# Attention on one core: seven pairs of exps' tiles added by DMAs, and a unit's side work in four blocks

## The chip, the cores and the metric

The kernel runs on one core of a Trainium2 chip. The metric is the device time of one execution in microseconds (us). TensorE (PE) multiplies, VectorE (DVE) and ScalarE (ACT) work elementwise, GpSimd (POOL) adds tiles and issues DMAs of its own, and SyncE (SP) issues the other DMAs.

## What is computed

x is 8 × 2048 × 256 and adj is 2048 × 2048, mostly zeros. Two layers follow each other, each with a residual and a LayerNorm:

```
x = layernorm(x + gcn(x, adj, ...))      # aggregation, two linears with batch norms
qkv = x @ W                              # 4 heads of 64
scores = q @ k.T / 8 + where(adj == 0, -inf, 0)
x = layernorm(x + softmax(scores) @ v)
```

The change touches only the second layer, the masked attention. Its softmax needs, for every query and head, the sum of the exps over all 2048 keys.

## The kernel before, in words

The attention works in 64 units: for each batch b (8), each pair of heads hp (2) and each chunk c of 512 queries (4). A unit has NT = 16 steps, one for each tile of 128 keys; g counts steps over all units. The order of the instructions on TensorE, VectorE, ACT and GpSimd is the order of the program text (the names in IN_ORDER), so each engine's queue can be read off the main loop at the end of attention().

One step g does the following. TensorE computes the scores of step g + 3 (scores, L838, tile st in PSUM; LEAD is 3). VectorE adds the mask (mask_scores, L850) and ACT takes the exp in place (exps, L856); the result is a tile prob of 128 keys × 2 heads × 512 queries, 512 KB, from a ring of 13. Then the step's side work is issued, then TensorE multiplies the prob of step g with v (weigh, L868, into out_ps), and add_up gives GpSimd the task of adding the tile to acc. In a unit's last step weigh comes before the masking, and finish_out copies and adds the two halves of out_ps (ACT L883, DVE L884), before that step's masking is queued.

The sums over keys: GpSimd adds the first NT − on_pe(u) tiles of a unit into acc. finish_sums then lets TensorE multiply acc, and each of the last on_pe(u) tiles, with ones (L895), which sums over the 128 partitions. on_pe is 1 in units 0 to 60 and 4 in units 61 to 63.

Side work is registered with at_step(u, j, f, ...): it runs in unit u at step int(j), in the order of j within the step. Its TensorE part stands between two groups of the step, and this text calls the side work of one step a block. It consists of:

- project (three for a unit: Q on w = 0, K on w = 1, L777; V on w = 2, L791), at the steps in PROJECT;
- finish_sums, finish_turn_sums (L909), finish_turn (L922) and finish (VectorE, L930) for the unit that ended before;
- in the four units in which a chunk of the next batch is made ready: norm, for two halves (y turned by TensorE, L711, then added to x on VectorE, L719, in add_y, with the LayerNorm statistics behind it), root (GpSimd), apply (ACT), and turn, for two halves (x1 turned by TensorE, L740, then copied to x1t by ACT, L746).

All of these use PSUM tiles named pm, from the pool ps_m with two buffers, in turn. A tile of it can be written again when its reader is done. The scores have two buffers (st) and out_ps one[...].

Before the change, a unit that prepares a chunk has blocks at step 0 (second y half, Q), 4 (sums), 6 (turned sums, K, turned output), 10 (first y half, V, first x1 half) and 13 (second x1 half). A unit that prepares none has those at 0, 4, 6 and 10 alone.

Of the kernel before, what the change touches and what calls it, by code (L numbers as in the profile page):

```python
# [8 lines left out]
F32 = mybir.dt.float32  # L9
U8 = mybir.dt.uint8  # L10
AF = mybir.ActivationFunctionType
ALU = mybir.AluOpType
# [14 lines left out]
def tile_gcn_then_masked_attention(  # L27
# [15 lines left out]
    nc = tc.nc  # L43
    ENG = mybir.EngineType
    PSUM = bass.MemoryType.PSUM
    P = 128
# [4 lines left out]
    NT = N // P  # L51
# [3 lines left out]
    CH = 512  # L55
    NCH = N // CH
# [140 lines left out]
    with tc.tile_pool(name="bt7", bufs=1, side="right") as bp7, tc.tile_pool(  # L197
        name="stage", bufs=2, side="right"
    ) as sp, tc.tile_pool(name="stage1", bufs=1, side="right") as sp1, tc.tile_pool(
        name="pst", bufs=4, space=PSUM  # L200
# [17 lines left out]
        for n, t in enumerate(order):  # L218
# [7 lines left out]
            j, m = divmod(t, HT)  # L226
            k, q = divmod(m, TPC)
            here = slice(q * P, (q + 1) * P)
            for g in range(NT // 4):
# [4 lines left out]
                i, m0 = divmod(4 * g, HT)  # L234
# [46 lines left out]
    with tc.tile_pool(  # L281
        name="psa", bufs=4, space=PSUM
    ) as psa, tc.tile_pool(name="psh", bufs=3, space=PSUM) as psh, tc.tile_pool(
        name="psd", bufs=1, space=PSUM
# [94 lines left out]
        for v, (k, b, d) in enumerate(units):  # L379
            first, last = v == 0, v == len(units) - 1  # L380
            turn = not last and units[v + 1][0] != k
            w = v + 1
# [99 lines left out]
        for n, (name, size) in enumerate((("h1", [P, NH, CH]), ("dbc", [P, N]))):  # L482
            t = lp.tile(size, F32, name=name)
            t = t if n else t.rearrange("p a b -> p (a b)")
# [156 lines left out]
    IT = BR // P  # L641
    NU = B * HP * NCH
# [34 lines left out]
    class Layer1Input:  # L677
# [37 lines left out]
        def add_y(self, b, c, half, pm, xt):  # L715
            tiles = range(IT * half, IT * (half + 1))
            here = slice(tiles[0], tiles[-1] + 1)
            t = self.x1[b, c]
            nc.vector.tensor_add(t[:, here], pm, xt[:, here])  # L719
            if half == 0:  # L720
                self.ln[b, c] = LayerNorm(self.pool, t)
            self.ln[b, c].stats(tiles)

        def root(self, b, c):
            self.ln[b, c].root(range(TPC))
# [83 lines left out]
    def attention():  # L809


        with tc.tile_pool(
# [9 lines left out]
            units = [(b, hp, c) for b in range(B) for hp in range(HP) for c in range(NCH)]  # L822
            probs, accs, outs, ots, sts, pms = {}, {}, {}, {}, {}, {}

            def on_pe(u):

                return 4 if u >= NU - NCH + 1 else 1

            def scores(g):
                u, j = divmod(g, NT)  # L830
# [40 lines left out]
                        )  # L871

            def add_up(g):
                u, j = divmod(g, NT)
                if j == 1:
                    accs[u] = ap_.tile([P, 2, CH], F32, name="acc")
                    nc.gpsimd.tensor_add(accs[u], probs[g - 1], probs[g])  # L877
                elif 1 < j < NT - on_pe(u):
                    nc.gpsimd.tensor_add(accs[u], accs[u], probs[g])  # L879

            def finish_out(u):
                ots[u] = ap_.tile([P, CH], F32, name="ot")
# [73 lines left out]
            def at_step(u, j, f, *args):  # L956
                tasks = side.setdefault((u, int(j)), [])
                tasks.append((j, f, args))
                tasks.sort(key=lambda task: task[0])

            per_b = HP * NCH
            for u in range(NU):
                b, hp, c = units[u]
                at_step(u + 1, 4, finish_sums, u)
                at_step(u + 1, 6, finish_turn_sums, u)
                at_step(u + 1, 6.2, finish_turn, u)
                at_step(u + 1, 6.2, finish, u, 0)
                at_step(u + 1, 7, finish, u, 1)
                if u == NU - 2:
                    for half in range(2):  # L970
                        at_step(u + 1, 8.3 + half, inp.emit_stats, b, c, half)
                        at_step(u + 1, 13 + half, inp.emit, b, c, half)
                    at_step(u + 1, 10.5, inp.root, b, c)
                elif u == NU - 1:
                    for half in range(2):
                        at_step(u + 1, 6.3 + half, inp.emit_stats, b, c, half)
                        at_step(u + 1, 6.4 + half, inp.root_half, b, c, half)
                        at_step(u + 1, 8 + half, inp.emit_half, b, c, half)
                    at_step(u + 1, 10, count_sums)
                elif hp == HP - 1:  # L980
                    for half in range(2):
                        at_step(u + 1, 10.3 + 3 * half, inp.emit_stats, b, c, half)
                        at_step(u + 2, 3 + half, inp.emit, b, c, half)
                    at_step(u + 2, 2, inp.root, b, c)

            PROJECT = (0.1, 6.1, 10.1)

            def project_at(u, b, hp, c):  # L990
                for w in range(3):
                    at_step(u, PROJECT[w], inp.project, b, hp, c, w)

            for b in range(B):
                u0 = b * per_b
                if b:
                    project_at(u0, b, 0, NCH - 1)
                for c in range(NCH):
                    project_at(u0 + 1 + c, b, 1, c)
                    if b + 1 == B:  # L1000
                        continue
                    u = u0 + 3 + c
                    at_step(u, 1, inp.load_y, b + 1, c)
                    at_step(u, 5, inp.load_x, b + 1, c)
                    for o in range(NO):
                        at_step(u, 5 + o, inp.bn, b + 1, c, o)
                    at_step(u, 10, inp.norm, b + 1, c, 0)
                    at_step(u + 1, 0, inp.norm, b + 1, c, 1)
                    at_step(u + 1, 4, inp.root, b + 1, c)
                    for half in range(2):  # L1010
                        at_step(u + 1, 7 + half, inp.apply, b + 1, c, half)
                        at_step(u + 1, 10.2 + 3 * half, inp.turn, b + 1, c, half)
                    if c < NCH - 1:
                        project_at(u + 2, b + 1, 0, c)

# [13 lines left out]
            with tc.manual_schedule(engines=IN_ORDER):  # L1029
                for c in range(NCH):  # L1030
                    inp.yt[0, c] = y0[c]
                    inp.x1[0, c] = ip.tile([P, TPC, D], F32, name="x1", bufs=NCH + 3)
                    for o in range(NO):
                        inp.bn(0, c, o)

                def ready(c):
                    pm = ps_s.tile([P, TPC, D], F32, name="st")
                    for half in range(2):
                        pmh = pm[:, half * IT : (half + 1) * IT, :]
                        inp.turn_y(0, c, half, pmh)  # L1040
                        inp.add_y(0, c, half, pmh, x0[c])
                    inp.root(0, c)

                def halves(f, c):
                    for half in range(2):
                        f(0, c, half)

                for c in range(NCH - 1):
                    ready(c)
                halves(inp.apply, 0)  # L1050
                halves(inp.turn, 0)
                halves(inp.apply, 1)
                inp.project(0, 0, 0, 1, k_on_act=True)
                inp.project(0, 0, 0, 0)
                ready(NCH - 1)
                right.close()
                ap_ = inp.y_pool = late.enter_context(
                    tc.tile_pool(name="attn", bufs=2, side="right", reuse_waits="tile")
                )
                inp.project(0, 0, 0, 2)  # L1060
                halves(inp.turn, 1)
                for g in range(LEAD):
                    mask_scores(g, scores(g))
                    exps(g)
                    if g == 1:
                        inp.project(0, 0, 1, 1)
                        halves(inp.apply, 2)
                for g in range(NU * NT):
                    u, j = divmod(g, NT)
                    ahead = g + LEAD < NU * NT  # L1070
                    if ahead:
                        st = scores(g + LEAD)
                    if j == NT - 1:
                        weigh(g)
                        finish_out(u)
                    if ahead:
                        mask_scores(g + LEAD, st)
                        exps(g + LEAD)
                    for _, f, args in side.get((u, j), ()):
                        f(*args)  # L1080
                    if j < NT - 1:
                        weigh(g)
                    add_up(g)
                for u in (NU, NU + 1):
                    for j in range(NT):
                        for _, f, args in side.get((u, j), ()):
                            f(*args)

    def attention_with_maxima():

        with tc.tile_pool(name="full", bufs=2) as ap_, tc.tile_pool(
# [9 lines left out]
            for b in range(B):  # L1101
                for c in range(NCH):
                    inp.load_y(b, c)
                    inp.load_x(b, c)
                    for o in range(NO):
                        inp.bn(b, c, o)
                    for half in range(2):
                        inp.norm(b, c, half)
                    inp.root(b, c)
                    for half in range(2):  # L1110
                        inp.apply(b, c, half)
                    for half in range(2):
                        inp.turn(b, c, half)
# [99 lines left out]
```

## Time and profile before

| | |
|---|---|
| time, median of 3 runs | 3622.35 us (3622.21 to 3624.46) |
| profiled execution | 3624.1 us, granted TensorE clock 0.995 |
| PE, POOL, DVE, ACT busy | 99%, 76%, 55%, 45% of the span |
| GpSimd adds into acc, L879 and L877 | 823 + 64, mean 2.37 us |
| sums on TensorE, L895 | 584 instructions for prob, 512 for acc |
| VectorE masking, L850 | 1024, mean 1.22 us |
| ACT exp, L856 | 1024, mean 1.06 us |
| a 512 KB store, out_dram<-x | 2.9 us from issue to landing |

A matmul of this type of data appears as two instructions, so a tile multiplied with ones has 8 of them. The mean of one instruction on TensorE says little, since four of the small tiles run beside each other; the timeline, with the start of one group after the other, is the better view. The busy shares are over the whole span. The attention begins near 1265 us, and in it GpSimd is busy nine tenths of the time.

### The profile page before, as it was taken

The page shows a single profiled execution, that of the slowest core. Times are in us where ns is not written, and L with a number is a line of the kernel's source. Part 1 is how long each engine was busy: PE and PEld are TensorE (multiplying, and loading weights), DVE is VectorE, ACT ScalarE, POOL GpSimd, SP SyncE. Part 2 cuts the span into 40 slices and gives each one's busy share as a digit, 9 for nine tenths or more (in the row PEclk, how much of TensorE's full clock was granted, in tenths as well). Part 3 has the DMA queues.
Part 4 walks back from the last instruction along what each step waited for, and adds up shares of the span by engine and source line. Part 5 has one row for each costly group of instructions (what it writes and reads, how often), then busy time and mean ns, then how long its engine had stood idle before and what let it go on. Part 6 is the DMA issues. An engine that isn't in the chain of part 4 may idle for free.

```text
span 3624.1 us, 55802 instructions
## 1 busy us (share of the span) xinstructions
PE 3585.2 (99%) x23055; PEld 1486.7 (41%) x23055; DVE 1988.9 (55%) x2929; ACT 1642.7 (45%) x2036; POOL 2761.0 (76%) x1461
## 2 busy tenths in 40 slices
PE   8999999999999899999999999999999999999998
PEld 5444444444444443433343433343343334343333
DVE  6212141221146656766766676676676677676666
ACT  5101100110135455665665665565566566556555
POOL 3543263424247678999999999999999999999997
PEclk9999999999999899999999999999999999999999
DMA  9122232231256300000010010010001001000000
GB/s 338 66 73 87 81 134 81 76 99 29 81 197 261 136 13 7 24 30 13 19 42 13 13 36 24 13 36 25 7 24 42 4 23 35 13 13 26 12 1 26
DMA packets 132777, 205.82 MB, mean 57 GB/s; under 512 B 6928, under 2 KB 113952, under 8 KB 122016
## 3 DMA queue, kind: packets, MB, share of 16 engines
q1 hardware_dynamic: 132048, 196.11, 15.8%
q0 software_dynamic: 288, 4.98, 0.4%
q8 instruction: 183, 3.00, 0.3%
q10 hardware_dynamic: 176, 1.06, 0.1%
q14 instruction: 82, 0.67, 0.1%
HBM read 126.62 MB, written 75.51 MB: 56 GB/s over the span
## 4 chain that ended last, share of the span: by engine, by line
PE 97%; DVE 1%; DMA 0%; ACT 0%; POOL 0%; issue 0%; POOLq 0%; ACTq 0%; SPq 0%; DVEq 0%
PE out_ps L868 25%; PE st L838 24%; PE pa L333 21%; PE pm L777 6%; PE ph L366 5%; PE pa L543 5%; PE pm L791 3%; PE pm L895 2%; PE pm L711 1%; PE pm L740 1%; PE pm L922 1%; PE ps L233 1%; PE pm L909 1%; PE ph L588 1%; DMA a<-in_adj_dram 0%; PE pc L243 0%
## 5 line engine op out<-in xcount | busy, mean ns | idle before, releaser
L879 POOL TENSOR_TENSOR acc<-acc,prob 128x1024 f32<-128x1024 f32 x823 | 1948.6, 2368 | 96.5 <-ACT prob L856 39.3
L850 DVE SCALAR_TENSOR_TENSOR prob<-mask,st 128x1024 f32<-128x1024 uint8 x1024 | 1242.7, 1219 | 605.3 <-PE st L838 551.2
L856 ACT ACTIVATE prob<-prob 128x1024 f32<-128x1024 f32 x1024 | 1082.4, 1057 | 943.7 <-DVE prob L850 923.6
L868 PE MATMUL out_ps<-prob,v 64*64 64x512 f32 x8192 | 1077.1, 596 | 1.7 <-DVE ot L884 1.7
L838 PE MATMUL st<-qt,kt 64*64 64x512 f32 x8192 | 1062.9, 589 | 0.1
L333 PE MATMUL pa<-t,x 128*128 128x512 f32 x1792 | 773.6, 594 | 2.7 <-ACT x L309 2.7
L838 PEld LDWEIGHTS st<-qt,kt 64*64 64x64 f32 x8192 | 312.6, 133 | 566.5 <-issue 527.0
L333 PEld LDWEIGHTS pa<-t,x 128*128 128x128 f32 x1792 | 341.4, 191 | 432.9 <-issue 428.9
L868 PEld LDWEIGHTS out_ps<-prob,v 64*64 64x64 f32 x8192 | 284.9, 132 | 511.5 <-issue 412.7
L414 POOL TENSOR_TENSOR ag<-ag,dbc 128x512 f32<-128x512 f32 x16 | 20.2, 1264 | 486.4 <-DVE ag L413 454.8
L370 ACT ACTIVATE h<-ph,b1s 128x512 f32<-128x512 f32 x112 | 76.9, 687 | 404.4 <-PE ph L366 404.4
L777 PE MATMUL pm<-x1t,wq 128*128 128x512 f32 x512 | 247.1, 606 | 0.7 <-ACT x1t L746 0.7
L394 ACT COPY ag<-pa 128x512 f32<-128x512 f32 x16 | 9.4, 586 | 423.1 <-PE pa L333 409.6
L366 PE MATMUL ph<-ag,w1s 128*128 128x512 f32 x448 | 193.4, 592 | 0.0
L877 POOL TENSOR_TENSOR acc<-prob 128x1024 f32<-128x1024 f32 x64 | 151.3, 2364 | 20.4 <-ACT prob L856 19.2
L672 ACT ACTIVATE x<-x,ln_nm,ln_rs 128x256 f32<-128x256 f32 x256 | 137.5, 586 | 8.0 <-POOL ln_nm L668 8.0
L371 DVE BATCH_NORM_STATS2 st<-h 128x6 f32<-128x512 f32 x112 | 76.8, 691 | 99.1 <-ACT h L370 99.1
L791 PEld LDWEIGHTS pm<-wq,x1t 128*128 128x128 f32 x1024 | 119.2, 192 | 28.5 <-issue 26.8
L366 PEld LDWEIGHTS ph<-ag,w1s 128*128 128x128 f32 x448 | 85.1, 190 | 107.1 <-issue 106.9
L791 PE MATMUL pm<-wq,x1t 128*128 128x128 f32 x1024 | 128.4, 278 | 0.0
L777 PEld LDWEIGHTS pm<-x1t,wq 128*128 128x128 f32 x512 | 88.1, 192 | 95.1 <-issue 88.3
L303 POOL TENSOR_TENSOR x<-x,dinv 128x1024 f32<-128x1024 f32 x60 | 116.8, 1968 | 0.0
(137 smaller groups left out, 2427.0 us busy)
## 6 DMA issues: line engine op xcount, KB each, us to landing
x<-in_x_dram SPq DMA_DIRECT2D x92, 512.0 KB, 4.2
h_d<-h SPq DMA_DIRECT2D x28, 1024.0 KB, 3.9
t<-h_d SPq DMA_DIRECT2D x28, 1024.0 KB, 8.0
a<-in_adj_dram SPq DMA_DIRECT2D x16, 1024.0 KB, 5.1
y_d<-ag SPq DMA_DIRECT2D x32, 512.0 KB, 2.6
out_dram<-x SPq DMA_DIRECT2D x31, 512.0 KB, 2.9
yt<-y_d SPq DMA_DIRECT2D x28, 512.0 KB, 3.2
bt_d<-t SPq DMA_DIRECT2D x4, 2048.0 KB, 13.2
```

The costliest lines, as they stand in the source:

```text
L333: nc.tensor.matmul(pa, s.t[:, m, :], t[:, m, :], start=(m == 0), stop=(m == HT - 1))
L366: nc.tensor.matmul(ph, w1s[:, d, f * P : (f + 1) * P], ag[:, d, :], start=(d == 0), stop=(d == ND - 1),)
L543: nc.tensor.matmul(py, w[:, f, :], t[:, f, :], start=(f == 0), stop=(f == 1))
L672: nc.scalar.activation(self.t[:, i, :], self.t[:, i, :], AF.Identity, bias=self.nm[:, i : i + 1], scale=self.rs[:, i : i + 1],)
L777: nc.tensor.matmul(pm, wq[:, d, wcols], xt[:, d, cols], start=(d == 0), stop=(d == ND - 1))
L791: nc.tensor.matmul(pm[:, j * P : (j + 1) * P], xt[:, d, t * P : (t + 1) * P], wq[:, d, wcols], start=(d == 0), stop=(d == ND - 1),)
L838: nc.tensor.matmul(st[r * HD : (r + 1) * HD, h, :], kt[hs, j * P + r * HD : j * P + (r + 1) * HD], qt[hs, cols], start=True, stop=True,)
L850: nc.vector.scalar_tensor_tensor(p, mask[:, j, cols][:, None, :].to_broadcast([P, 2, CH]), MASKED, st, op0=ALU.mult, op1=ALU.add,)
L856: nc.scalar.activation(probs[g], probs[g], AF.Exp)
L868: nc.tensor.matmul(outs[u][hs, r, :], inp.qkv[b, hp][2][rs, j, hs], probs[g][rs, h, :], start=(j == 0), stop=(j == NT - 1),)
L877: nc.gpsimd.tensor_add(accs[u], probs[g - 1], probs[g])
L879: nc.gpsimd.tensor_add(accs[u], accs[u], probs[g])
```

## The change

It has two parts. First, GpSimd no longer adds every tile by itself: tiles 0 and 1, 2 and 3, and so on to 12 and 13 (PAIRS) are added pairwise by accumulating DMAs, issued by GpSimd at the pair's second step. The add of the pair's sum into acc is queued four steps after. With this GpSimd has eight adds in a unit for fourteen, and on_pe goes to 0 in all units but the last: TensorE multiplies acc alone with ones.

Second, the side work is put together in fewer blocks: both y halves stand around the Q projection at step 0, both x1 halves around the V projection at step 11, and the statistics of y get a method of their own, stats_y, at steps 1 and 2. The sums move to step 5, beside the K projection, and the turned sums and output to step 8. Loads, batch norm and output move to match.

```diff
             t = self.x1[b, c]
             nc.vector.tensor_add(t[:, here], pm, xt[:, here])
+
+        def stats_y(self, b, c, half):
             if half == 0:
-                self.ln[b, c] = LayerNorm(self.pool, t)
-            self.ln[b, c].stats(tiles)
+                self.ln[b, c] = LayerNorm(self.pool, self.x1[b, c])
+            self.ln[b, c].stats(range(IT * half, IT * (half + 1)))
...
+            PAIRS = range(0, NT - 2, 2)
+
             def on_pe(u):
-                return 4 if u >= NU - NCH + 1 else 1
+                return 4 if u == NU - 1 else 0
...
             def add_up(g):
                 u, j = divmod(g, NT)
-                if j == 1:
-                    accs[u] = ap_.tile([P, 2, CH], F32, name="acc")
-                    nc.gpsimd.tensor_add(accs[u], probs[g - 1], probs[g])
-                elif 1 < j < NT - on_pe(u):
+                here = NT - on_pe(u)
+                if j - 1 in PAIRS and j < here:
+                    nc.gpsimd.dma_start(probs[g - 1], probs[g], accum_op=ALU.add)
+                elif PAIRS[-1] + 1 < j < here:
                     nc.gpsimd.tensor_add(accs[u], accs[u], probs[g])
+
+                v, i = divmod(g - 5, NT)
+                if v < 0 or i not in PAIRS[1:] or i + 1 >= NT - on_pe(v):
+                    return
+                if i == PAIRS[1]:
+                    accs[v] = ap_.tile([P, 2, CH], F32, name="acc")
+                    nc.gpsimd.tensor_add(accs[v], probs[g - 7], probs[g - 5])
+                else:
+                    nc.gpsimd.tensor_add(accs[v], accs[v], probs[g - 5])
...
-                at_step(u + 1, 4, finish_sums, u)
-                at_step(u + 1, 6, finish_turn_sums, u)
-                at_step(u + 1, 6.2, finish_turn, u)
-                at_step(u + 1, 6.2, finish, u, 0)
-                at_step(u + 1, 7, finish, u, 1)
+                at_step(u + 1, 5, finish_sums, u)
+                at_step(u + 1, 8, finish_turn_sums, u)
+                at_step(u + 1, 8.1, finish_turn, u)
+                at_step(u + 1, 8.2, finish, u, 0)
+                at_step(u + 1, 9, finish, u, 1)
...
-                        at_step(u + 1, 10.3 + 3 * half, inp.emit_stats, b, c, half)
-                        at_step(u + 2, 3 + half, inp.emit, b, c, half)
-                    at_step(u + 2, 2, inp.root, b, c)
-            PROJECT = (0.1, 6.1, 10.1)
+                        at_step(u + 1, 12 + 2 * half, inp.emit_stats, b, c, half)
+                        at_step(u + 2, 6.3 + half, inp.emit, b, c, half)
+                    at_step(u + 2, 3, inp.root, b, c)
+            PROJECT = (0.1, 5.1, 11.1)
...
-                    at_step(u, 1, inp.load_y, b + 1, c)
-                    at_step(u, 5, inp.load_x, b + 1, c)
+                    at_step(u, 2, inp.load_y, b + 1, c)
+                    at_step(u, 8, inp.load_x, b + 1, c)
                     for o in range(NO):
-                        at_step(u, 5 + o, inp.bn, b + 1, c, o)
-                    at_step(u, 10, inp.norm, b + 1, c, 0)
-                    at_step(u + 1, 0, inp.norm, b + 1, c, 1)
-                    at_step(u + 1, 4, inp.root, b + 1, c)
+                        at_step(u, 11.3 + 2 * o, inp.bn, b + 1, c, o)
                     for half in range(2):
-                        at_step(u + 1, 7 + half, inp.apply, b + 1, c, half)
-                        at_step(u + 1, 10.2 + 3 * half, inp.turn, b + 1, c, half)
+                        at_step(u + 1, 0.2 * half, inp.norm, b + 1, c, half)
+                        at_step(u + 1, 1 + 1.5 * half, inp.stats_y, b + 1, c, half)
+                        at_step(u + 1, 8.5 + half, inp.apply, b + 1, c, half)
+                        at_step(u + 1, 11 + 0.2 * half, inp.turn, b + 1, c, half)
+                    at_step(u + 1, 4.5, inp.root, b + 1, c)
```

The first batch, which is made ready before the units begin, calls stats_y behind each norm half, as before.

More of the change, by code (lines that the diff above doesn't have):

```diff
@@ L963, in attention @@
                 b, hp, c = units[u]
-                at_step(u + 1, 4, finish_sums, u)
-                at_step(u + 1, 6, finish_turn_sums, u)
-                at_step(u + 1, 6.2, finish_turn, u)
-                at_step(u + 1, 6.2, finish, u, 0)
-                at_step(u + 1, 7, finish, u, 1)
+                at_step(u + 1, 5, finish_sums, u)
[3 more added lines that the diff above has]
+                at_step(u + 1, 9, finish, u, 1)
                 if u == NU - 2:
                     for half in range(2):
-                        at_step(u + 1, 8.3 + half, inp.emit_stats, b, c, half)
+                        at_step(u + 1, 9.3 + half, inp.emit_stats, b, c, half)
                         at_step(u + 1, 13 + half, inp.emit, b, c, half)
@@ L975, in attention @@
                     for half in range(2):
[L976 to L979, printed above, removed]
+                        at_step(u + 1, 8.3 + half, inp.emit_stats, b, c, half)
+                        at_step(u + 1, 8.4 + half, inp.root_half, b, c, half)
+                        at_step(u + 1, 10 + half, inp.emit_half, b, c, half)
+                    at_step(u + 1, 12, count_sums)
                 elif hp == HP - 1:
                     for half in range(2):
-                        at_step(u + 1, 10.3 + 3 * half, inp.emit_stats, b, c, half)
-                        at_step(u + 2, 3 + half, inp.emit, b, c, half)
-                    at_step(u + 2, 2, inp.root, b, c)
-            PROJECT = (0.1, 6.1, 10.1)
+                        at_step(u + 1, 12 + 2 * half, inp.emit_stats, b, c, half)
+                        at_step(u + 2, 6.3 + half, inp.emit, b, c, half)
+                    at_step(u + 2, 3, inp.root, b, c)
+            PROJECT = (0.1, 5.1, 11.1)
             def project_at(u, b, hp, c):
                 for w in range(3):
-                    at_step(u, PROJECT[w], inp.project, b, hp, c, w)
+                    early = 1 if w == 2 and (hp, c) == (0, NCH - 1) else 0
+                    at_step(u, PROJECT[w] - early, inp.project, b, hp, c, w)
             for b in range(B):
@@ L1041, in ready @@
                         inp.add_y(0, c, half, pmh, x0[c])
+                        inp.stats_y(0, c, half)
                     inp.root(0, c)
@@ L1108, in attention_with_maxima @@
                         inp.norm(b, c, half)
+                        inp.stats_y(b, c, half)
                     inp.root(b, c)
```

## Prediction

> **What bounds the kernel now.** I read the chain of work that ended last first:
>
> ```profile
> PE 97%; DVE 1%; DMA 0%; ACT 0%; POOL 0%; issue 0%; POOLq 0%; ACTq 0%; SPq 0%; DVEq 0%
> ```
>
> TensorE alone sets the end. The change lies in the attention (from about 1265 us to the end), so I read TensorE's timeline there, over one unit in which the next batch is prepared. Columns: start, duration, engine, line, operation, tiles, count.
>
> ```profile
> 2019.30 1.04 PE L838 MATMUL st<-qt,kt 64*64 64x512 f32 x8
> 2020.27 0.66 PE L711 MATMUL pm<-ident,yt 128*128 128x128 f32 x4
> 2020.76 1.88 PE L777 MATMUL pm<-x1t,wq 128*128 128x512 f32 x4
> 2022.57 1.09 PE L868 MATMUL out_ps<-prob,v 64*64 64x512 f32 x8
> ...
> 2029.60 0.64 PE L895 MATMUL pm<-prob,ones 128*32 128x256 f32 x8
> 2030.05 0.61 PE L895 MATMUL pm<-acc,ones 128*32 128x256 f32 x8
> 2030.60 1.09 PE L868 MATMUL out_ps<-prob,v 64*64 64x512 f32 x8
> ...
> 2044.24 1.95 PE L791 MATMUL pm<-wq,x1t 128*128 128x128 f32 x16
> 2046.03 0.60 PE L740 MATMUL pm<-ident,x 128*128 128x128 f32 x4
> 2046.56 1.09 PE L868 MATMUL out_ps<-prob,v 64*64 64x512 f32 x8
> ...
> 2050.90 1.04 PE L838 MATMUL st<-qt,kt 64*64 64x512 f32 x8
> 2051.87 0.66 PE L740 MATMUL pm<-ident,x 128*128 128x128 f32 x4
> 2052.45 1.09 PE L868 MATMUL out_ps<-prob,v 64*64 64x512 f32 x8
> 2053.36 1.04 PE L838 MATMUL st<-qt,kt 64*64 64x512 f32 x8
> ```
>
> There is no bracket with an idle time: everything starts as the work before it ends. So the time is the sum of TensorE's work, and a change can shorten it only by removing TensorE work, and lengthens it by every wait it puts into TensorE's queue. Last, what the other queues do beside it (DVE, then ACT):
>
> ```profile
> 2020.16 0.69 DVE L884 TENSOR_TENSOR ot<-out_ps,ot 128x512 f32<-128x512 f32 x1 [1.90 <-ACT ot L883]
> 2020.77 2.34 DVE L850 SCALAR_TENSOR_TENSOR prob<-mask,st 128x1024 f32<-128x1024 uint8 x2
> 2023.03 0.68 DVE L719 TENSOR_TENSOR x<-pm,x 128x512 f32<-128x512 f32 x1
> ```
>
> ```profile
> 2045.20 1.06 ACT L856 ACTIVATE prob<-prob 128x1024 f32<-128x1024 f32 x1 [0.19 <-DVE prob L850]
> 2046.23 0.59 ACT L798 COPY v<-pm 128x512 f32<-128x512 f32 x1
> ```
>
> The reader is to see that the add of a y half at a unit's first step (L719) ends at 2023.71, long after its transposes, because a sum and two maskings stand before it; and that the first copy out of PSUM in the block at step 10 ends at 2046.82, because an exp stands before it. Today nothing on TensorE waits for either.
>
> **What the Trainium skill says.** "DMA: Bandwidth & Descriptors", section "SWDGE vs HWDGE vs iDMA": accumulation in a DMA is to be had from GpSimd alone, whose software writes the descriptors. So each added DMA takes GpSimd time. The trace has two DMAs of GpSimd, 0.97 us (wq, L632) and 0.58 us (mask, L633). "Collectives: The Full Stack", section "The bandwidth ceiling: the fold count and why AG ≠ RS ≠ AR": a reducing transfer reads two sources through the same ring and so runs at about half a copy's rate; no accumulating DMA is in the trace of before. "TensorEngine Tiling (Array Packing)", section "Key Properties": a change of the tiling mode drains TensorE. The trace agrees: after a block of side work the L868 group takes 0.16 us more than 0.86 on the chain of waits (1.02).
>
> **The change, part by part.**
>
> *Fewer tiles summed on TensorE.* finish_sums puts exps' tiles through ones: one in units 0 to 60, four in 61 to 63, 73 in all (the row of prob,ones has x584, 8 for each). Afterwards only unit 63 keeps its four, so 69 go. One costs 2030.05 − 2029.60 = 0.45 us; a five-tile group at the end takes 2.30 us on the chain, 0.46 each. 69 × 0.45 = 31 us, all on the bounding engine: **−31.0**.
>
> *GpSimd.* A unit had 14 adds at 2.43 us (19.48 us for 8 in a row), 34 us; it gets 8 adds (19.5) and 7 DMA issues at 0.58 to 0.97 each (4 to 7 us; I take 1), plus 1.8 us of LayerNorm roots: 28 us of a unit of 35.5 to 37.5. The list of waits has no TensorE row that waits for GpSimd, so this is worth nothing; it makes the first part possible. The accumulation (512 KB): a store of that size lands in 2.9 us here; the skill's fit of 2.0 us plus bytes over 436 GB/s ("Anatomy of one DMA"), with the bytes twice, gives an estimate of 4.4 us; upper bound 5.8, twice the store. I take 4.4. The add that needs it stands four steps later (4 × 1.72 = 6.9 us or more), and behind it GpSimd's next adds and issues. The last add of a unit comes after step 1 of the next one, ends by step 3, and finish_sums (the only TensorE work behind it) is at step 5. A tile of exps comes back after 13 steps and its masking runs three steps ahead: tile 0 is wanted at step 10, its add stands at step 7. Cost: 0.
>
> *Blocks.* The unit above has five blocks of side work; the fifth is the lone x1 half at 2051.87. It costs 2053.36 − 2050.90 = 2.46 against 1.72 for a bare step: 0.74. Afterwards the two x1 halves take the first and the last place around the V projection, where a y half and an x1 half were (no difference), and a y half goes behind the Q projection at step 0. Appended transposes cost 0.43: L791 to the next L868 is 2.32 with them (2044.24 to 2046.56) and 1.89 without (2007.92 to 2009.81). Net 0.31 in each unit that has such a block: 7 batches × 4 chunks = 28. **−8.7**. The other moves leave four blocks as four: 0, since TensorE does the same work in them.
>
> *Two new waits.* ps_m has two pm buffers. "Around a projection" makes a block take three: half, projection, half. The third reuses the first's, and waits for its reader.
> Step 0, y halves: the reader is the add, L719, in a place the trace already shows: behind the ot sum, which waits for ACT's copy of the ended unit, and two maskings. It ends at 2023.71; DVE to TensorE takes 0.06 (the y halves' start-up: an add ends at 1254.68, L711 starts at 1254.74). So 2023.77. Without a wait the second half would start 1.72 after the projection (L777 to L922 in the block at step 6), 2022.48. Wait 1.29 us. Taking the statistics out of add_y doesn't help this one: they stood behind the add.
> Step 11, x1 halves: the reader is ACT's copy to x1t, behind the exp of the same step, whose masking can't start before the scores end. The trace has a copy in exactly this place, the v copy ending at 2046.82; plus 0.06 is 2046.88, against the L740 start at 2046.03. Wait 0.85 us. ACT has no backlog there: applies move from steps 7 and 8 to 8 and 9, as far before the block as they were.
> Behind both waits stand the product with v and the next scores, that is everything. Nothing gives the time back, since TensorE has no idle time later. 28 × (1.29 + 0.85) = **+59.9**.
>
> Sum: −31.0 − 8.7 + 59.9 = +20.2. From 3622.35: 3643.
>
> **The rivals.**
> *No waits, faster.* If the readers were done in time, only the savings stay: 3622.4 − 39.7 = 3583. For: VectorE is busy 55% and ACT 45%, and a projection of 1.72 us is longer than an add or a copy. Against: the order in these queues, which the traced times already contain. If only the wait on ACT is real: 3583 + 28 × 0.85 = 3607; only the one on VectorE: 3583 + 28 × 1.29 = 3619.
> *Accumulating DMAs become the bound.* At 5.8 us each without overlap, seven take 40.6 us, over a unit's 35.1 (35.5 of a unit without preparation, 1585.53 to 1621.06 between ot sums, less 0.45) or 38.9 (37.5 − 0.76 + 2.14). 35 × 5.5 + 28 × 1.7 = 240: 3883 with the waits. For: no such DMA was ever seen in this trace. Against: much of 2.9 us is latency, which overlaps; the estimate for the moving of bytes alone is 2.4 us, 17 us a unit.
>
> **How the numbers follow.** Both waits: 0.68, at 3643; each wait may be wrong by 0.2 us, TensorE's ends being modelled, and a stopped TensorE may need up to 0.1 to start again: 3631 to 3657. Only VectorE's wait: 0.08 (3619, within 0.2%). Only ACT's: 0.08 (3607, faster). None: 0.08 (3583). DMAs as the bound: 0.08 (slower). So slower 0.76, same 0.08, faster 0.16. The range takes in the first three: 3605 to 3658.
>
> **What would show it.** The sums' group with 68 × 8 = 544 instructions for 1,096, and no idle time before it for GpSimd. In a preparing unit, TensorE idle before the second L711 of step 0 (1.2 to 1.4 us, released by the add) and before the second x1 half of step 11 (0.8 to 1.0 us, by the copy to x1t), 28 times each; four blocks; units of 38.9 us, the others 35.1. DMA rows of about 1 us on GpSimd, with no wait over 1 us before the adds that follow. Wrong if those two idle times are under half of this, or if GpSimd's adds wait for DMAs and maskings wait for GpSimd.

## The result, and the profile after

The change makes the kernel slower: 3665.1 us (3662.56 to 3665.77, 4 runs) against 3623.4 us (4 runs), a ratio of 1.0113 with a 95% interval of 1.0096 to 1.0131. The forecast was 3643, the range 3605 to 3658: the direction was right, the size half of what came, and the time is outside the range. The spans of the two profiled executions are 3663.5 and 3624.1 us, 39.4 apart; this is the sum that the readings below have to explain.

The chain of work that ended last, by engine, from the page of the kernel after:

```profile
PE 89%; DVE 6%; ACT 3%; issue 1%; POOL 1%; DMA 0%; DVEq 0%; POOLq 0%; ACTq 0%; SPq 0%
```

TensorE had 97% of this chain and has 89%; VectorE (1% before), ACT and GpSimd (both 0%) have 6, 3 and 1%, which they can only have where TensorE waits for them. TensorE's busy time went down, from 3585.2 to 3570.8 us, while the span went up. TensorE's timeline in a unit that prepares a chunk shows where (start, duration, what; a bracket gives idle time and what ended it):

```profile
2004.13 1.04 PE L844 MATMUL st<-qt,kt 64*64 64x512 f32 x8
2005.10 0.64 PE L911 MATMUL pm<-acc,ones 128*32 128x256 f32 x8
2005.67 1.98 PE L779 MATMUL pm<-x1t,wq 128*128 128x512 f32 x4
2007.58 1.09 PE L874 MATMUL out_ps<-prob,v 64*64 64x512 f32 x8
2008.49 1.04 PE L844 MATMUL st<-qt,kt 64*64 64x512 f32 x8
...
2030.23 1.88 PE L779 MATMUL pm<-x1t,wq 128*128 128x512 f32 x4
2033.24 0.66 PE L711 MATMUL pm<-ident,yt 128*128 128x128 f32 x4 [1.13 <-DVE x L719]
...
2056.97 1.95 PE L793 MATMUL pm<-wq,x1t 128*128 128x128 f32 x16
2059.60 0.66 PE L742 MATMUL pm<-ident,x 128*128 128x128 f32 x4 [0.68 <-ACT x1t L748]
```

The two brackets are the two new waits. Counted from start to start, as the prediction did, the second y half begins 2033.24 − (2030.23 + 1.72) = 1.29 us late and the second x1 half 2059.60 − (2056.97 + 1.79) = 0.84 us late. The queues ahead of their readers, VectorE's and then ACT's timeline:

```profile
2029.63 0.69 DVE L900 TENSOR_TENSOR ot<-out_ps,ot 128x512 f32<-128x512 f32 x1 [1.97 <-ACT ot L899]
2030.24 2.34 DVE L856 SCALAR_TENSOR_TENSOR prob<-mask,st 128x1024 f32<-128x1024 uint8 x2
2032.50 0.68 DVE L719 TENSOR_TENSOR x<-pm,x 128x512 f32<-128x512 f32 x1
```

```profile
2057.93 1.06 ACT L862 ACTIVATE prob<-prob 128x1024 f32<-128x1024 f32 x1 [0.41 <-DVE prob L856]
2058.96 0.59 ACT L748 COPY x1t<-pm 128x512 f32<-128x512 f32 x1
```

The add stands behind the ot sum and two maskings, the copy behind the exp, each in the place that the trace of before showed. All 28 chunks look like this. The list of waits sums them up (engine and line, what it waited for, us in total, times, longest):

```profile
PE pm L711 <- DVE x L719: 31.6, 28, 1.1
PE pm L742 <- ACT x1t L748: 17.3, 28, 0.7
```

These two waits were forecast. The 20 us that were not are mostly in two other places. One has no bracket and is seen in the distance between the ot sums of one unit and the next, here called the unit's length: a unit without preparation took 35.53 us and takes 35.29, which is 0.24 saved and not 0.45. The other is the end of the kernel, on the timeline of all engines (L97 begins the LayerNorm root):

```profile
3637.47 0.23 POOL L97 TENSOR_SCALAR ln_rs<-ln_mv 128x4 f32<-128x4 f32 x1 [1.25 <-DVE ln_mv L662]
...
3639.68 0.92 POOL L884 DMA_DIRECT2D prob<-prob  x1 [0.27 <-ACT prob L862]
3640.36 7.49 POOL L895 TENSOR_TENSOR acc<-acc,prob 128x1024 f32<-128x1024 f32 x3
...
3641.82 1.93 PE L911 MATMUL pm<-prob,ones 128*32 128x256 f32 x32
...
3647.90 0.64 PE L911 MATMUL pm<-acc,ones 128*32 128x256 f32 x8 [4.14 <-POOL acc L895]
```

In the last unit GpSimd does the LayerNorm root of the unit before, then issues the last DMA, and has three adds left behind it; TensorE has nothing but their sum to go on with and waits 4.14 us. The root itself starts late: it waits 1.25 us for VectorE's statistics, which the change put one step later in this unit (emit_stats, from steps 8.3 and 9.3 to 9.3 and 10.3; the diff above leaves these lines out).

What each part came to, from the two profiled executions (before, after):

| part | forecast, us | measured, us | from |
|---|---|---|---|
| waits and merged blocks, 28 chunks | +51.2 | +52.4 | four preparing units and the one before them: 185.53 less 5 × 35.53, and 191.82 less 5 × 35.29; 1.87 a chunk |
| sums in units 1 to 60 | −27.0 | −14.4 | 60 × (35.29 − 35.53) |
| units 61 to 63 (nine tiles) | −4.0 | −3.0 | 30.67 + 31.96 + 30.11 to 30.24 + 30.24 + 29.25 |
| after the last ot sum | 0 | +4.8 | 15.46 to 20.28 |

They add up to +39.8; the first ot sum, 0.6 us earlier, brings it near 39.4. Of unit 63's four tiles only 0.86 us is seen: its last four products with v take 4.36 us (3637.46 to 3641.82) where they took 3.63, since TensorE now comes to them before the last exps are done.

### The profile page after: what moved, and what is told of

The parts are those of the page before. It is cut to its first block, busy times and chain, and to the rows that moved or that the text cites. A ratio compares the mean times of both kernels' runs of the same rounds, so it can differ in the third digit from the quotient of the medians.

```text
span 3663.5 us, 55125 instructions
## 1 busy us (share of the span) xinstructions
PE 3570.8 (97%) x22503; PEld 1469.3 (40%) x22503; DVE 1986.7 (54%) x2929; ACT 1641.5 (45%) x2036; POOL 2269.2 (62%) x1530
## 4 chain that ended last, share of the span: by engine, by line
PE 89%; DVE 6%; ACT 3%; issue 1%; POOL 1%; DMA 0%; DVEq 0%; POOLq 0%; ACTq 0%; SPq 0%
PE out_ps L874 23%; PE st L844 22%; PE pa L333 21%; PE ph L366 5%; PE pm L779 5%; PE pa L543 5%; DVE prob L856 4%; PE pm L793 2%; ACT prob L862 2%; PE pm L911 1%; PE pm L938 1%; PE pm L925 1%; PE ps L233 1%; PE pm L742 1%; DVE x L719 1%
## 5 line engine op out<-in xcount | busy, mean ns | idle before, releaser
L895 POOL TENSOR_TENSOR acc<-acc,prob 128x1024 f32<-128x1024 f32 x319 | 830.5, 2603 | 6.1 <-DMA prob<-prob 1.0
L884 POOL DMA_DIRECT2D prob<-prob x447 | 398.7, 901 | 625.3 <-PE out_ps L874 502.4
L886 POOL TENSOR_TENSOR acc<-acc,prob 128x1024 f32<-128x1024 f32 x126 | 297.6, 2362 | 9.9
L893 POOL TENSOR_TENSOR acc<-prob 128x1024 f32<-128x1024 f32 x64 | 171.4, 2679 | 3.2 <-DMA prob<-prob 3.2
L793 PEld LDWEIGHTS pm<-wq,x1t 128*128 128x128 f32 x1024 | 119.2, 192 | 28.5 <-issue 21.1
L793 PE MATMUL pm<-wq,x1t 128*128 128x128 f32 x1024 | 128.4, 278 | 0.0
```

The source lines that it names most:

```text
L793: nc.tensor.matmul(pm[:, j * P : (j + 1) * P], xt[:, d, t * P : (t + 1) * P], wq[:, d, wcols], start=(d == 0), stop=(d == ND - 1),)
L884: nc.gpsimd.dma_start(probs[g - 1], probs[g], accum_op=ALU.add)
L895: nc.gpsimd.tensor_add(accs[v], accs[v], probs[g - 5])
```

## Experiments

### The two parts one by one: dma_alone and side_alone

Two theories stood against each other for the missing 20 us: the K projection's new place and the last unit (theory 1), or the DMAs themselves (theory 2). dma_alone is the kernel before with after's add_up, PAIRS and on_pe, side_alone is the kernel after with before's:

```diff
 # dma_alone, on before
-                return 4 if u >= NU - NCH + 1 else 1
+                return 4 if u == NU - 1 else 0
 ...                                   # and add_up of the kernel after
```

> The kernel before with the DMA part alone: pairs added by DMAs, one tile fewer through ones; side work at its old steps. Theory 1 (the 19 us that the prediction missed come from the K projection's new place, 12 us, and from the last unit's adds, 5 us; the DMAs cost TensorE nothing): 31 us saved on TensorE, 5 us given back in the last unit, 26 us less than before, about 3597. Theory 2 (the accumulating DMAs themselves take the missing time, by traffic in SBUF or by GpSimd's slower adds): 31 - 19 = 12 us less, about 3611.

> The kernel after with before's sums: GpSimd adds every tile, one tile through ones; the new steps of the side work stay. Theory 1: the waits and blocks cost 28 x 1.87 = 52 us as in the trace of after, and K's place 0.2 us in 61 units, 12 us: 65 us more than before, about 3688. Theory 2: waits and blocks alone, 52 us more, about 3675.

side_alone: 3691.1 us, 1.0178 (1.0161 to 1.0195). Theory 1 had 3688, theory 2 3675. So the side work costs 67 us by itself (before had 3624.45 in these runs), more than waits and blocks: a unit without preparation, which has neither, takes 35.73 us for 35.53.

dma_alone: 3609.9 us, 0.9956 (0.9940 to 0.9973). This is theory 2's number, and the trace shows that it is not theory 2's cause. Most units have 35.10 or 37.07 us against 35.53 and 37.50, the full 0.43 saved, so that DMA traffic takes nothing from TensorE. But some are 0.7 us longer than these. In such a unit (timeline of all engines):

```profile
2201.91 2.65 POOL L890 TENSOR_TENSOR acc<-acc,prob 128x1024 f32<-128x1024 f32 x1
...
2204.65 0.23 POOL L97 TENSOR_SCALAR ln_rs<-ln_mv 128x4 f32<-128x4 f32 x1
...
2206.63 1.09 ACT L672 ACTIVATE x<-x,ln_nm,ln_rs 128x256 f32<-128x256 f32 x2 [0.80 <-POOL ln_nm L668]
...
2209.56 0.35 ACT L914 COPY sm<-pm 128x256 f32<-128x256 f32 x1
...
2209.96 0.44 PE L920 MATMUL pm<-ident,sm 128*128 128x128 f32 x2 [0.67 <-ACT sm L914]
```

ACT waits for GpSimd, whose LayerNorm root now stands behind an add of the last pair, so the applies come late, and the copy of the sums behind them: TensorE waits for that, 13 times for 9.9 us (one of the 13, 0.5 us behind everything else, is in the kernel before too). In units 61 to 63 it waits 0.5 us a unit for acc too, and 2.96 us at the end; there the statistics have their old steps, and the root does not wait for them. At their old steps the sums and the output stand too near to GpSimd's new, later work. In the kernel after, where they stand at steps 5, 8 and 6.3, none of these waits is left but those at the end; which of the moves is needed was not tested.

### The K projection: k_back and k_before_sums

```diff
 # k_back, on after
-            PROJECT = (0.1, 5.1, 11.1)
+            PROJECT = (0.1, 8.05, 11.1)
 # k_before_sums, on after
-                at_step(u + 1, 5, finish_sums, u)
+                at_step(u + 1, 5.2, finish_sums, u)
```

> The kernel after with the K projection at step 8, between the turned sums and the turned output, as before the change; the sums stand alone at step 5. Theory 1 (a projection that ends a block, and stands behind the sums' tiling, costs 0.2 us more than one between transposes): 61 x 0.2 = 12 us less than after, about 3653. Theory 2: no change, 3665.

> The kernel after with K and sums swapped within step 5: the projection first, the sums last. Theory 1 (a projection that ends a block costs about 0.2 us more than one inside, and the sums at the end cost 0.55): up to 0.2 us in 61 units, 12 us less than after, 3653. Theory 2 (the cost is the change of tiling between the sums' 128 by 32 tiles and the projection's 128 by 128, whichever comes first): 3662 to 3665.

k_back: 3652.6 us, 1.0073 (1.0056 to 1.0090), 12.5 less than after, as expected. Units of 35.29 become 35.10, those of 39.11 become 38.92. 60 units have a K projection, not 61; between the first and the last ot sum the gain is 11.7 us; the rest of the 12.5 lies outside the units. Two rows of step 8 in k_back:

```profile
1864.63 1.88 PE L779 MATMUL pm<-x1t,wq 128*128 128x512 f32 x4
1866.35 0.60 PE L938 MATMUL pm<-ident,ot 128*128 128x128 f32 x4
```

From the projection's start to the next group's it is 1.72 us; at step 5 of after, above, it is 1.91 (2005.67 to 2007.58).

k_before_sums: 3663.7 us, 1.0107 (1.0090 to 1.0124), and no unit's length changes. So it is not that a projection ends the block. TensorE's timeline of k_before_sums, to be set beside step 5 of after above:

```profile
2003.28 1.04 PE L844 MATMUL st<-qt,kt 64*64 64x512 f32 x8
2004.25 1.98 PE L779 MATMUL pm<-x1t,wq 128*128 128x512 f32 x4
2006.17 0.64 PE L911 MATMUL pm<-acc,ones 128*32 128x256 f32 x8
2006.74 1.09 PE L874 MATMUL out_ps<-prob,v 64*64 64x512 f32 x8
2007.64 1.04 PE L844 MATMUL st<-qt,kt 64*64 64x512 f32 x8
```

From scores to scores it is 4.36 us in both orders. What is common to both is the number of changes of tiling, the way in which a group divides TensorE into parts: the 128*32, 128*128 and 64*64 in the rows. Sums alone and K between the turns make four changes for these two blocks (64, 32, 64, 128, 64); sums beside K make five (64, 32, 128, 64, 128, 64), in either order. The fifth costs the 0.19 us. The step lengths, from scores to scores, bear the count out in a third place. A projection of this kind adds 1.72 us where it brings no change of tiling (4.40 between the turns in k_back, 2.68 for the turns without it in after), 1.91 where it brings one (4.36 beside the sums, 2.45 for the sums alone in k_back), and 2.07 where it brings two (3.79 for Q alone in its step, 1.72 for a bare step). The Trainium skill, "TensorEngine Tiling (Array Packing)", "Key Properties", says that switching the mode drains TensorE; the runs agree, and put 0.16 to 0.19 us on one switch.

### The waits: y_early and first_halves_early

The first half of a block that has two goes ahead of the step's masking and exp in all queues, TensorE's order staying as it is:

```diff
                     if ahead:
                         st = scores(g + LEAD)
...
+                    tasks = side.get((u, j), ())
+                    first = [t for t in tasks if t[0] == j and t[1] in (inp.norm, inp.turn,)]
+                    for _, f, args in first:
+                        f(*args)
                     if ahead:
                         mask_scores(g + LEAD, st)
                         exps(g + LEAD)
```

y_early has inp.norm alone in that list.

> The kernel after with the first y half alone issued before its step's masking; the x1 halves stay. Theory (the two waits add up, 28 x 1.1 for y and 28 x 0.85 for x1, the latter kept by 7 of its 28 in the kernel with both moved): 28 x 1.1 = 31 us less than after, about 3634. Rival (the waits share slack, so that one alone takes less than half of the 49 us that both took): 3645 or more.

> The kernel after with one move: in a step that begins with a first half (y at step 0, x1 at step 11) this half is issued before the step's masking and exp, so its reader stands ahead of them. Theory 1 (the waits are those of the reader's place in its queue): the x1 wait of 0.85 us goes, of the y wait of 1.29 us some 0.2 stay, since one masking still stands ahead: 28 x 1.94 = 54 us less than after, about 3611. Rival: the delayed masking or exp becomes TensorE's next wait and takes back over half of it, 3640 or more.

y_early: 3633.6 us, 1.0024 (1.0015 to 1.0032), 31.5 less than after. first_halves_early: 3615.7 us, 0.9974 (0.9964 to 0.9984), 49.4 less. The waits add up, and neither comes back elsewhere. Most of the 5 us short of 54 have a cause that nobody had seen. TensorE's timeline of first_halves_early still has the x1 wait, but only in the first chunk of each batch, 7 of 28, and ACT's timeline tells why:

```profile
2044.43 0.65 PE L742 MATMUL pm<-ident,x 128*128 128x128 f32 x4 [0.68 <-ACT x1t L748]
```

```profile
2043.79 0.59 ACT L748 COPY x1t<-pm 128x512 f32<-128x512 f32 x1 [1.44 <-PE pm L793]
```

The copy to x1t waits for the V projection (L793) of the batch that ends, since x1t has one buffer and that projection is its last reader. The new order puts the first x1 half ahead of the last read. In the kernel after this wait is hidden under the other.

### The last unit: plain_last and last_six

plain_last gives the last unit's tiles to GpSimd one by one, as before the change; last_six leaves the pairs and gives TensorE two tiles more.

```diff
 # plain_last, on after, in add_up
+                if u == NU - 1:
+                    if j == 1:
+                        ...            # acc from the first two tiles
+                    elif 1 < j < here:
+                        nc.gpsimd.tensor_add(accs[u], accs[u], probs[g])
+                elif ...
 # last_six, on after
-                return 4 if u == NU - 1 else 0
+                return 6 if u == NU - 1 else 0
```

> The kernel after, but the last unit's tiles are added one by one by GpSimd, as before the change, not in pairs by DMAs. Theory (in the last unit the last sum waits 4.1 us for three adds queued behind the last DMA issue): with two adds left after the LayerNorm root, as before, 3 to 5 us less than after, about 3661. Rival (the sum waits for the root's statistics whatever is queued): no change, 3665.

> The kernel after with six of the last unit's tiles put through ones on TensorE for four, so that one pair's add fewer is left to GpSimd behind the LayerNorm root. Theory (in the last unit the sum waits for GpSimd's queue: root, DMA issue, three adds): the wait of 4.1 us goes, two more tiles cost 0.9: about 3 us less than after, 3662. Rival: the wait stays since the root comes late anyway: 3665 or more.

plain_last went wrong: 3670.0 us, 1.0123 (1.0106 to 1.0139), 5 more than after. GpSimd, from its own timeline, now adds without a pause and comes to the root at 3645.72, where the kernel after had 3637.47:

```profile
3628.61 17.03 POOL L888 TENSOR_TENSOR acc<-acc,prob 128x1024 f32<-128x1024 f32 x7
3645.72 0.23 POOL L97 TENSOR_SCALAR ln_rs<-ln_mv 128x4 f32<-128x4 f32 x1
```

Eleven adds of 2.4 us don't fit into a unit of 29 us that begins with the leftovers of the one before. Before the change GpSimd had none of these leftovers. The pairs are worth keeping; what has to go is the last one.

last_six: 3660.0 us, 1.0099 (1.0083 to 1.0114), 5 less than after where 3 were expected; the list of waits of its TensorE has no entry for acc any more. The 2 us between forecast and gain are within the spread of the runs.

### The parts together: all_four and combined

all_four joins first_halves_early, k_back and plain_last, and in a batch's first chunk puts the x1 halves behind V (step 11.2) and at step 13. combined is the same with last_six in place of plain_last:

```diff
-                        at_step(u + 1, 11 + 0.2 * half, inp.turn, b + 1, c, half)
+                        at_step(
+                            u + 1, 11 + 0.2 * half if c else 11.2 + 2 * half,
+                            inp.turn, b + 1, c, half,
+                        )
```

> The best version that the findings give: the kernel after with both first halves issued before masking and exp, K back between the turned sums and output, the last unit added by GpSimd alone, and in a batch's first chunk the x1 halves behind the V projection and at step 13 (its x1t buffer is still read by that projection). From the 3616 of the kernel with both halves moved: 12.6 for K, 4 for the last unit, 7 x 0.55 for the first chunk: about 3595. Rival (K between the turns runs into the other moves as the DMAs alone did into the old steps, with new waits): 3605 or more.

> The kernel after with both first halves issued before masking and exp, K between the turned sums and output, the first chunk's x1 halves behind V and at step 13, and six tiles through ones in the last unit. From the 3605.5 of the version whose last unit GpSimd added alone: less its 9.7 us of waits in the last unit, plus 0.9 for two tiles: about 3597. Rival: the last unit gives back what it gave before, 3602 or more.

all_four: 3605.6 us, 0.9949 (0.9932 to 0.9966). Its units are as hoped for (35.10, and 36.97 to 37.33 with preparation), and its last two waits for acc come to 9.7 us, as they did in plain_last (9.5). So the number is the rival's, and the cause is not: it is the last unit, and no wait has come in with K. combined: 3593.9 us, 0.9918 (0.9904 to 0.9931), faster than both kernels. Its list of waits for TensorE from 1300 us to 3600, whole:

```profile
PE pm L961 <- DVE ot L957: 4.7, 1, 4.7
PE out_ps L874 <- DVE ot L900: 1.7, 3, 0.6
PE pm L925 <- ACT sm L919: 0.5, 1, 0.5
PE out_ps L874 <- ACT prob L862: 0.3, 1, 0.3
```

Both L711 and L742 are gone from it, and so is acc. The first row is the check of all sums behind everything else, which before had too (4.67 us). The list is as short as that of before; the gain is TensorE work left out.

But a piece of the y wait is still there, and no list shows it (PE, then DVE):

```profile
1433.63 1.88 PE L779 MATMUL pm<-x1t,wq 128*128 128x512 f32 x4
1435.51 0.66 PE L711 MATMUL pm<-ident,yt 128*128 128x128 f32 x4
```

```profile
1434.77 0.68 DVE L719 TENSOR_TENSOR x<-pm,x 128x512 f32<-128x512 f32 x1
```

The second y half starts 0.06 us after the end of the add, as it did where it waited in plain sight, and 1.88 us after the projection's start, not 1.72. The row of the projection, whose end is modelled, fills these 0.16 us, so that there is no idle time to list. This is the 0.2 us that the expectation of first_halves_early left standing; in 28 chunks it comes to some 4.5 us, by the same reading.

## Why the prediction was right or wrong

- **TensorE is the bound, so a wait put into its queue is paid in full.** Right. y_early and first_halves_early take out most of the waits and get that much back, 31.5 and 49.4 us.
- **The two new waits, 1.29 and 0.85 us, 28 times.** Right to 0.01 us. They could be read off before the change, since the trace of before had the same instructions in the same places of the queues.
- **Merged blocks, 0.31 us a chunk.** Right: waits and blocks together were put at 1.83 us a chunk and are 1.87. From scores to scores, the three steps concerned took 4.18, 4.69 and 2.47 us before and take 5.97, 5.50 and 1.72; less the waits of 2.13 that is 0.28 us saved.
- **69 tiles at 0.45 us, 31 us.** The size is right where it can be seen alone: k_back's units are 35.53 − 35.10 = 0.43 shorter than before's. The step that failed is the one after: "The other moves leave four blocks as four: 0, since TensorE does the same work in them." The count of blocks stays, but K beside the sums is one change of tiling more, 0.19 us in each of 60 units, which k_back gets back (11.7 of its 12.5 us). The trace of before had the number that tells it: 0.16 us for the group after a block. I had quoted that a change of tiling costs, and then counted blocks instead of changes.
- **GpSimd, "Cost: 0".** Right in 60 units of the kernel after, and on the DMAs: they land in 4.7 us (estimate 4.4), the issue takes 0.90 us (taken as 1), and TensorE waits for none; GpSimd's own adds do three times, 1.0 to 2.1 us, in the last units. (The halved rate that the prediction took from the Trainium skill is stated there for a ring of several cores; carrying it over to a DMA within one core was an inference, which 4.7 us fits and doesn't prove.) The cost of 0 failed in the last unit, where no next unit's step 5 gives GpSimd time: 4.8 us at the end, 4.14 of them TensorE's wait for acc. I had followed GpSimd's queue through a unit in the middle and not through the last. It was also too simple in another way: dma_alone shows that the lateness of GpSimd would have cost some 10 us had the sums and the output stayed at their steps.
- **The wait of the first x1 half on the old x1t** wasn't seen; it cost nothing in the kernel after and 5 us as soon as the other wait was gone.
- **The range.** It took in errors of 0.2 us in the waits, which were right, and 0.1 us for a stopped TensorE to start again, of which the 1.87 us a chunk have no sign; it took in none in the savings, which were not right.
- **The rivals.** "No waits" and "DMAs become the bound" fell, the latter by dma_alone's units without a wait, which are 0.43 us shorter.

What stays open: last_six gained 5 us against 4.1 of wait less 0.9 of work, and combined 3 us more than expected. Both are within what one kernel's runs differ by here: 2 to 5 us, and 6.5 in the thirteen of y_early. combined's five runs are three near 3593.8 and two near 3597, and its median falls among the three. That the last unit's wait comes in part from the later statistics, and not from the three adds alone, was read from the traces and not tested by itself.

## What to carry to other kernels

When one engine is busy all the time, go through its queue and ask of every instruction that takes a buffer who reads that buffer last, and what stands ahead of that reader in the reader's own queue; the trace of the old kernel can have the same queue, and here it gave the wait to a hundredth of a us. A list of waits without such a row is no proof that there is none: compare the starts, since a modelled end can cover the gap. For work moved on TensorE count the changes of tiling, not the blocks. And follow a side engine's queue through the last round as well, where no later round hides what it still owes.

## What the runs showed of the hardware that was not expected

- An accumulating DMA of 512 KB within SBUF lands in 4.7 us (median of 447), against 2.9 us for a store of that size in the kernel before, and occupies GpSimd for 0.90 us. With seven in a unit the DMA engines are busy five to six tenths of the time, and TensorE's matmuls keep their means of 596 and 589 ns.
- GpSimd's adds are listed at 2.60 us on average (L895) against 2.37 before. The add behind a DMA issue is the one that is longer: its row starts 0.62 us after that of the issue, which is 0.87 long, so that the two overlap by about 0.25 us. Plain adds beside them (L886) stay at 2.36.
- One change of tiling more costs TensorE 0.16 to 0.19 us, whichever of the two groups comes first.
